# The state's two products moved onto 32-column groups of the array, in one row with the products of scores and v

## The chip, the cores and the metric

The kernel runs on one core of one Trainium2 chip. The metric is the time of one execution on the device, in microseconds; smaller is better. The kernel before took 1318.28 us as the median of three runs (1317.63 to 1319.15).

## The reference

The input `x` has 8 sequences of 1024 tokens with 256 features, in float32. It is normalised, and two things that read the normalised `xn` are added to it: a linear attention with 16 heads of 16 features, and a mixture of 8 experts of which each token uses 2.

```
q = elu(xn @ Wq.T) + 1 ; k = elu(xn @ Wk.T) + 1 ; v = xn @ Wv.T        # 16 heads of 16
kv_cumsum = cumsum over tokens of k[d] * v[e]                          # per head, 16 x 16
k_cumsum  = cumsum over tokens of k
out   = sum over d of q[d] * kv_cumsum[d, e]
denom = clip(sum over d of q[d] * k_cumsum[d], 1e-6)
x + (out / denom) @ Wo.T + sum over the 2 chosen experts of weight * (silu(xn @ W1) * (xn @ W3)) @ W2
```

The running sum `kv_cumsum` is what this change is about. It is never formed token by token. The tokens are cut into chunks of 128; within a chunk the masked scores q.k are multiplied with v, and what all earlier chunks of the sequence contribute is q times a state, the sum of k times v over those chunks.

## The kernel before

The 8192 tokens form 16 blocks of 512 tokens (two blocks to a sequence), and each block has four chunks of 128. Features lie across partitions in two halves (`KC` = 2, index `hh`), each with 8 heads, or 4 pairs of heads of 32 features (`PAIR`). Everything is float32, and one float32 matmul of the program appears in the profile as two records.

The experts' work is cut into tiles of 128 tokens that share an expert. The main loop has one iteration for each such tile, 132 in all. An iteration fetches the tile's rows and the expert's weights ahead of time, multiplies with W1 and W3 (`gu_ps`, L1216, 16 matmuls), transposes the next tile (`xg_t`, L1183), and multiplies the previous tile with W2 (`y_ps`, L1235). Ahead of this the iteration makes one step of the attention, sometimes two (`attend_upto`). Each block has nine steps: four that project q, k and v and prepare the denominator, one for the first chunk's scores, and four in which `block_steps` calls `scores` of the next chunk, `attend` of the last one (the product with Wo, `a_ps`, L979) and `weigh` of the present one. Two steps are made together only at certain places of a block (`TOGETHER`).

`scores(t, c)` multiplies k and q (`s_ps`, L919, on groups of 32 rows of the array, 8 matmuls) into four banks; VectorE masks each bank for causality (L926) and so frees it. Then, unless the chunk is the last of its sequence, it multiplies k and v (`kv_ps`, L934): two matmuls, one for each half, with 128 columns of k held in the array and 128 columns of v streamed. Of each 128 by 128 result only the 16 by 16 squares on the diagonal, one for each head, are wanted; VectorE multiplies with the mask `heads` (L939) and adds the state so far (L941), and the sum is the new state. The old state, `before_c`, goes with the chunk.

`weigh(t, c, ...)` fills one result `o_ps` of 128 partitions by 2 x 128. First come the products of q and the old state (L953): two matmuls over the whole array. Onto them it adds the products of masked scores and v (L960): 16 matmuls of 32 columns each, one column group for each pair of heads in a half, so that four of them stand side by side in the array. VectorE multiplies with the reciprocal denominator (L967) into `oT`.

Results of the array lie in three pools of banks: four for `s_ps` and `gu_ps`, two for `y_ps` and `a_ps`, and two for `kv_ps`, `o_ps` and the transposes. The start of the kernel (up to the first iterations) is written in a fixed order; after it, a scheduler decides the order of the instructions on TensorE, VectorE and ScalarE, within each engine's queue, and the engines work their queues in order. Weight transfers are issued from SP, in the order of the program.

Of the kernel before, what the change touches and what calls it, by code (L numbers as in the profile page):

```python
# [46 lines left out]
F32 = mybir.dt.float32  # L47
# [3 lines left out]
ALU = mybir.AluOpType  # L51
AX = mybir.AxisListType

P = 128
# [3 lines left out]
PAIR = 2 * HD  # L58
# [5 lines left out]
def tile_attention_moe(  # L64
# [14 lines left out]
    nc = tc.nc  # L79
    B, L, H = x.shape  # L80
    E, _, I = w1.shape
    KC = H // P
    IC = I // P
    TB = 512
    NCH = TB // P
    N = B * L
    NBLK = N // TB
    BLK_PER_SEQ = L // TB
# [22 lines left out]
    three = ctx.enter_context(tc.tile_pool(name="three", bufs=3))  # L111
# [3 lines left out]
    ps_t = ctx.enter_context(tc.tile_pool(name="ps_t", bufs=2, space=bass.MemoryType.PSUM))  # L115
# [114 lines left out]
    heads = const.tile([P, P], F32, name="heads")  # L230
# [16 lines left out]
    va = const.tile([P, NCH, HALF, 2, PAIR], F32, name="va")  # L247
# [12 lines left out]
        nc.gpsimd.tensor_copy(own_of[:, o, o * HALF : (o + 1) * HALF], own)  # L260

    causal_b = causal.unsqueeze(1).to_broadcast([P, 4, P])
    heads_b = heads.unsqueeze(1).to_broadcast([P, KC, P])


    lgs = {}
# [116 lines left out]
    new = f_one.tile([P, E, MOST], F32, name="new")  # L383
# [384 lines left out]
    def own_v(va, c, a, b):  # L768

        pairs = va[:, c, a:b].rearrange("p g s d -> p g (s d)")  # L770
        return pairs.rearrange("p g (q d) -> p g q d", d=HD)[:, :, 0:4:3, :]
# [135 lines left out]
    state = [None]  # L907

    def scores(t, c):

        qT, qm, kT, kn, va, rden = blocks[t]
        first = t % BLK_PER_SEQ == 0 and c == 0
        last = t % BLK_PER_SEQ == BLK_PER_SEQ - 1 and c == NCH - 1
        span = bass.ts(c, P)
        s_ps = [ps_mm.tile([P, KC, 2, P], F32, tag="mm", name="s_ps") for r in range(4)]
        for hh in range(KC):
            for r in range(4):
                rows = slice(32 * r, 32 * r + 32)
                nc.tensor.matmul(  # L919
                    s_ps[r][:, hh].rearrange("p a l -> p (a l)"), lhsT=kT[rows, hh, span],  # L920
                    rhs=qm[rows, hh, :, span], start=True, stop=True,
                )
        s_sb = []
        for r in range(4):
            sm = masked.tile([P, KC * 2, P], F32, tag="s_sb", name="s_sb")
            nc.vector.tensor_tensor(  # L926
                sm, s_ps[r].rearrange("p k a l -> p (k a) l"), causal_b, ALU.mult
            )
            s_sb.append(sm)
        before_c = state[0]  # L930
        if not last:
            kv_ps = ps_t.tile([P, KC, P], F32, tag="t", name="kv_ps")
            for hh in range(KC):
                nc.tensor.matmul(  # L934
                    kv_ps[:, hh, :], lhsT=kn[:, c, bass.ts(hh, P)],
                    rhs=own_v(va, c, 4 * hh, 4 * hh + 4), start=True, stop=True,
                )
            new = three.tile([P, KC, P], F32, tag="kv", name="kv")
            nc.vector.tensor_tensor(new, kv_ps, heads_b, ALU.mult)  # L939
            if not first:  # L940
                nc.vector.tensor_tensor(new, new, before_c, ALU.add)  # L941
            state[0] = new
        return t, c, s_sb, before_c

    def weigh(t, c, s_sb, before_c):

        qT, qm, kT, kn, va, rden = blocks[t]
        first = t % BLK_PER_SEQ == 0 and c == 0
        span = bass.ts(c, P)
        o_ps = ps_t.tile([P, KC, P], F32, tag="t", name="o_ps")  # L950
        if not first:
            for hh in range(KC):
                nc.tensor.matmul(  # L953
                    o_ps[:, hh, :], lhsT=before_c[:, hh, :], rhs=qT[:, hh, span],
                    start=(hh == 0), stop=False, skip_group_check=True,
                )
        for hh in range(KC):
            for a in range(2):
                for r in range(4):
                    nc.tensor.matmul(  # L960
                        o_ps[32 * r : 32 * r + 32, hh, :],
                        lhsT=va[:, c, 4 * hh + r, a, :],
                        rhs=s_sb[r][:, 2 * hh + a, :],
                        start=(first and a == 0), stop=(a == 1), skip_group_check=True,
                    )
        oT = two.tile([P, KC, P], F32, tag="oT", name="oT")
        nc.vector.tensor_tensor(oT, rden[:, c], o_ps, ALU.mult)  # L967
        return oT

    ats = {}  # L970
# [24 lines left out]
    def block_steps(t):  # L995


        for i, _ in enumerate(project(t)):
            if i == 1 and behind:
                attend(*behind.pop())  # L1000
            if i in (1, 3, 5, 8):
                yield
        if t + 1 < NBLK:
            fetch(t + 1)
        waiting = scores(t, 0)
        yield
        done = None
        for c in range(NCH):
            coming = scores(t, c + 1) if c + 1 < NCH else None
            if done and c + 1 < NCH:  # L1010
                attend(*done)
            oT = weigh(*waiting)
            if done and c + 1 == NCH:
                attend(*done)
            done = t, c, oT
            waiting = coming
            if c + 1 < NCH or t + 1 < NBLK:
                yield
        behind.append(done)
        if t + 1 == NBLK:  # L1020
            attend(*behind.pop())
            yield
# [24 lines left out]
    with tc.manual_schedule(engines={EN.DVE, EN.Activation, EN.PE, EN.Pool}):  # L1047
# [63 lines left out]
        for _ in range(2):  # L1111
            idle_ps = ps_mm.tile([P, TB], F32, tag="mm", name="idle_ps")
            nc.tensor.matmul(
                idle_ps, lhsT=ident, rhs=blocks[0][0][:, 0, :], start=True, stop=True
# [170 lines left out]
    for j in range(NM + 1):  # L1285
        if j + 1 < NM:
            ffn_norm(j + 1)
        t = FB + j
# [27 lines left out]
        if LISTS <= j < LISTS + NBLK - FB:  # L1316
            t = FB + j - LISTS
# [66 lines left out]
```

## Time and profile before

| what | value |
|---|---|
| median of three runs | 1318.28 us |
| profiled execution, whole | 1329.68 us |
| its span | 1328.0 us |
| granted TensorE clock, mean | 0.989 |
| TensorE busy in the span | 1270.6 us, 96% |
| VectorE busy | 636.9 us, 48% |
| ScalarE busy | 526.1 us, 40% |
| GpSimd busy | 523.1 us, 39% |
| `kv_ps`, L934: 224 records | 40.0 us busy |
| `o_ps` from the state, L953: 224 records | 34.9 us busy |
| `o_ps` from scores and v, L960: 2048 records | 73.2 us busy |
| `s_ps`, L919: 1024 records | 85.5 us busy |

PE is TensorE's matmul side and PEld its weight loads, which run beside the matmuls; DVE is VectorE, ACT ScalarE, POOL GpSimd. A line of the timeline gives the start of a group of equal instructions, its duration, the engine, the line of the code, the operation with its result and operands, the number of rows by columns of the array in use, the moving operand (partitions by elements) and the count; in brackets, the engine's idle time before it and what ended that. The ends of matmuls are modelled and overlap with what follows, so that distances between starts tell more than durations.

### The profile page before, as it was taken

The page shows a single profiled execution, that of the slowest core. Times are in us where ns is not written, and L with a number is a line of the kernel's source. Part 1 is how long each engine was busy: PE and PEld are TensorE (multiplying, and loading weights), DVE is VectorE, ACT ScalarE, POOL GpSimd, SP SyncE. Part 2 cuts the span into 40 slices and gives each one's busy share as a digit, 9 for nine tenths or more (in the row PEclk, how much of TensorE's full clock was granted, in tenths as well). Part 3 has the DMA queues.
Part 4 walks back from the last instruction along what each step waited for, and adds up shares of the span by engine and source line. Part 5 has one row for each costly group of instructions (what it writes and reads, how often), then busy time and mean ns, then how long its engine had stood idle before and what let it go on. Part 6 is the DMA issues. An engine that isn't in the chain of part 4 may idle for free.

```text
span 1328.0 us, 28290 instructions
## 1 busy us (share of the span) xinstructions
PE 1270.6 (96%) x10968; PEld 1092.2 (82%) x10968; DVE 636.9 (48%) x1436; ACT 526.1 (40%) x1060; POOL 523.1 (39%) x460
## 2 busy tenths in 40 slices
PE   5689999999999999999999999999999999999996
PEld 4478887787888888888888888898888888888886
DVE  7667489764252434435343535344443525243441
ACT  4466364461524325161525243341515152433411
POOL 3633333233254443443443525343434334343432
PEclk9899999999999999999999999999999999999998
DMA  9688576466685766666675757476676767575763
GB/s 340 229 276 258 154 200 170 130 173 206 176 229 141 198 166 155 189 173 172 169 190 145 216 132 208 126 188 171 160 186 170 189 153 194 147 198 134 198 161 72
DMA packets 163462, 240.36 MB, mean 181 GB/s; under 512 B 16098, under 2 KB 87394, under 8 KB 163042
## 3 DMA queue, kind: packets, MB, share of 16 engines
q1 hardware_dynamic: 119938, 184.31, 45.0%
q0 software_dynamic: 38064, 43.22, 19.3%
q10 hardware_dynamic: 5328, 11.01, 2.3%
q8 instruction: 90, 1.47, 0.5%
q14 instruction: 42, 0.34, 0.1%
HBM read 196.30 MB, written 52.67 MB: 187 GB/s over the span
## 4 chain that ended last, share of the span: by engine, by line
PE 87%; DVE 7%; ACT 2%; issue 1%; DMA 1%; another core or an unknown queue 1%; POOL 0%; POOLq 0%; DVEq 0%; ACTq 0%
PE gu_ps L1216 34%; PE y_ps L1235 16%; PE o_ps L960 5%; PE s_ps L919 5%; PE a_ps L979 4%; PE zq L795 4%; PE zkk L811 4%; PE zkv L811 4%; PE kv_ps L934 2%; PE o_ps L953 2%; PE xg_t L1183 2%; DVE s_sb L926 1%; PE tp L333 1%; PE den L880 1%; PE tp L858 1%
## 5 line engine op out<-in xcount | busy, mean ns | idle before, releaser
L1216 PE MATMUL gu_ps<-xgT,w 128*128 128x128 f32 x4224 | 511.2, 278 | 8.9 <-DVE s_sb L926 7.6
L1216 PEld LDWEIGHTS gu_ps<-xgT,w 128*128 128x128 f32 x4224 | 492.5, 193 | 28.8 <-issue 12.5
L1162 POOL DMA_INDIRECT xg<-in_x_dram,src_i x132 | 128.1, 970 | 406.1 <-ACT xgT L1185 322.4
L1246 POOL DMA_INDIRECT out_dram<-y,dst_i x107 | 176.3, 1648 | 222.2 <-DVE kn L765 54.2
L1235 PE MATMUL y_ps<-w_sb,hT 128*128 x1056 | 250.6, 380 | 2.6 <-DVE hT L1227 2.0
L1227 DVE TENSOR_TENSOR hT<-gu_ps,hT 128x512 f32<-128x512 f32 x132 | 91.1, 690 | 274.4 <-PE gu_ps L1216 198.0
L1235 PEld LDWEIGHTS y_ps<-w_sb,hT 128*128 128x128 f32 x1056 | 190.2, 190 | 24.0 <-DVE hT L1227 1.9
L1224 ACT ACTIVATE hT<-gu_ps 128x512 f32<-128x512 f32 x132 | 78.8, 597 | 299.9 <-PE gu_ps L1216 255.0
L926 DVE TENSOR_TENSOR s_sb<-s_ps,causal 128x512 f32<-128x512 f32 x256 | 163.6, 684 | 54.0 <-PE s_ps L919 25.5
L1242 DVE TENSOR_SCALAR y<-y_ps,entry 128x256 f32<-128x256 f32 x132 | 63.5, 481 | 120.0 <-PE y_ps L1235 75.0
L1167 POOL DMA_INDIRECT entry<-tab_d,of_i x107 | 106.5, 995 | 32.6 <-issue 30.5
L1185 ACT COPY xgT<-xg_t 128x256 f32<-128x256 f32 x132 | 49.0, 371 | 145.2 <-PE xg_t L1183 141.7
L984 ACT COPY at<-a_ps 128x256 f32<-128x256 f32 x64 | 23.7, 370 | 159.2 <-PE a_ps L979 149.0
L919 PE MATMUL s_ps<-qm,kT 32*128 32x256 f32 x1024 | 85.5, 405 | 0.5 <-DVE hT L1227 0.4
L1174 ACT ACTIVATE xg<-xg,entry 128x256 f32<-128x256 f32 x132 | 79.6, 603 | 3.4 <-issue 3.4
L960 PE MATMUL o_ps<-s_sb,va 128*32 128x128 f32 x2048 | 73.2, 276 | 0.0
L919 PEld LDWEIGHTS s_ps<-qm,kT 32*128 32x128 f32 x1024 | 51.0, 184 | 24.2 <-issue 19.6
L979 PE MATMUL a_ps<-wo_sb,oT 128*128 128x256 f32 x256 | 69.0, 393 | 0.1
L1246 POOL DMA_INDIRECT acc_d<-y,src_i x25 | 44.0, 1761 | 55.2 <-DVE y L1242 15.4
L960 PEld LDWEIGHTS o_ps<-s_sb,va 128*32 128x32 f32 x2048 | 53.2, 109 | 9.8 <-DVE oT L967 0.8
L811 PE MATMUL zkk<-wkv_sb,xnT 128*128 128x256 f32 x256 | 60.0, 384 | 0.0
L795 PE MATMUL zq<-xnT,wq_sb 128*128 128x512 f32 x128 | 59.9, 609 | 0.0
(211 smaller groups left out, 1361.7 us busy)
## 6 DMA issues: line engine op xcount, KB each, us to landing
w<-in_w_dram SPq DMA_DIRECT2D x264, 512.0 KB
den_d<-over SPq DMA_DIRECT2D x64, 128.0 KB
rden<-den_d SPq DMA_DIRECT2D x16, 512.0 KB
xnT_d<-xnT ACTq DMA_DIRECT2D x15, 512.0 KB
xnT<-xnT_d SPq DMA_DIRECT2D x15, 512.0 KB
out_dram<-in_x_dram SPq DMA_DIRECT2D x12, 512.0 KB
out_dram<-at POOLq DMA_DIRECT2D x12, 512.0 KB
xb<-in_x_dram SPq DMA_DIRECT2D x10, 512.0 KB
```

What stands on the lines that cost most here:

```text
L795: nc.tensor.matmul(z, lhsT=wq_sb[:, k, bass.ts(o, P)], rhs=xnTs[t][:, k, :], start=(k == 0), stop=(k == KC - 1),)
L811: nc.tensor.matmul(z[:, i, :], lhsT=xnTs[t][:, k, bass.ts(c + i, P)], rhs=wkv_sb[:, k, a, :], start=(k == 0), stop=(k == KC - 1),)
L919: nc.tensor.matmul(s_ps[r][:, hh].rearrange("p a l -> p (a l)"), lhsT=kT[rows, hh, span], rhs=qm[rows, hh, :, span], start=True, stop=True,)
L926: nc.vector.tensor_tensor(sm, s_ps[r].rearrange("p k a l -> p (k a) l"), causal_b, ALU.mult)
L960: nc.tensor.matmul(o_ps[32 * r : 32 * r + 32, hh, :], lhsT=va[:, c, 4 * hh + r, a, :], rhs=s_sb[r][:, 2 * hh + a, :], start=(first and a = ...
L979: nc.tensor.matmul(a_ps, lhsT=oT[:, hh, :], rhs=wo_sb[:, hh, :], start=(hh == 0), stop=(hh == 1),)
L1162: nc.gpsimd.indirect_dma_start(out=xg[j], out_offset=None, in_=x_rows[:, :], in_offset=bass.IndirectOffsetOnAxis(ap=src_i[:, i : i + 1], a ...
L1167: nc.gpsimd.indirect_dma_start(out=entry[j], out_offset=None, in_=table[:, :], in_offset=bass.IndirectOffsetOnAxis(ap=num_i[:, i : i + 1], ...
L1216: done = nc.tensor.matmul(ps[:, i, :], lhsT=w13[:, k, bass.ts(i, P)], rhs=xgT[j][:, k, :], start=(k == 0), stop=(k == KC - 1),)
L1227: nc.vector.tensor_tensor(hT, gu[1], hT, ALU.mult)
L1235: done = nc.tensor.matmul(y_ps, lhsT=hT[:, i, :], rhs=w2_sb[:, bass.ds(e * (IC * H) + i * H, H)], start=(i == 0), stop=(i == IC - 1),)
L1246: nc.gpsimd.indirect_dma_start(out=rows[:, :], out_offset=bass.IndirectOffsetOnAxis(ap=dst_i[:, i : i + 1], axis=0), in_=ys.pop(j), in_off ...
```

## The change

The product of k and v moves from `scores` to `weigh`, behind the products of scores and v, and is computed only where it is wanted: for each pair of heads, 32 columns of k against the 32 columns of v of the same pair, eight matmuls in place of two, each on its own group of 32 columns of the array. The result has 2 x 32 columns in place of 2 x 128 and shares one tile, and one bank, with `o_ps`. VectorE spreads it over 128 columns while it multiplies with the mask. The product of q and the old state is likewise cut into eight matmuls of 32 columns. The state is now read and replaced within `weigh`; the instructions of VectorE for the new state stand behind the one that makes `oT`.

```diff
@@ scores
-        before_c = state[0]
-        if not last:
-            kv_ps = ps_t.tile([P, KC, P], F32, tag="t", name="kv_ps")
-            for hh in range(KC):
-                nc.tensor.matmul(
-                    kv_ps[:, hh, :], lhsT=kn[:, c, bass.ts(hh, P)],
-                    rhs=own_v(va, c, 4 * hh, 4 * hh + 4), start=True, stop=True,
-                )
-            new = three.tile([P, KC, P], F32, tag="kv", name="kv")
-            nc.vector.tensor_tensor(new, kv_ps, heads_b, ALU.mult)
-            if not first:
-                nc.vector.tensor_tensor(new, new, before_c, ALU.add)
-            state[0] = new
-        return t, c, s_sb, before_c
+        return t, c, s_sb
@@ weigh
-        o_ps = ps_t.tile([P, KC, P], F32, tag="t", name="o_ps")
+        both_ps = ps_t.tile([P, KC * P + KC * PAIR], F32, tag="t", name="o_ps")
+        o_ps = both_ps[:, 0 : KC * P].rearrange("p (k l) -> p k l", k=KC)
+        kv_ps = both_ps[:, KC * P :].rearrange("p (k d) -> p k d", k=KC)
+        before_c = state[0]
         if not first:
             for hh in range(KC):
-                nc.tensor.matmul(
-                    o_ps[:, hh, :], lhsT=before_c[:, hh, :], rhs=qT[:, hh, span],
-                    start=(hh == 0), stop=False, skip_group_check=True,
-                )
+                for r in range(4):
+                    nc.tensor.matmul(
+                        o_ps[32 * r : 32 * r + 32, hh, :],
+                        lhsT=before_c[:, hh, 32 * r : 32 * r + 32], rhs=qT[:, hh, span],
+                        start=(hh == 0), stop=False, skip_group_check=True,
+                    )
...
+        if not last:
+            for hh in range(KC):
+                for r in range(4):
+                    nc.tensor.matmul(
+                        kv_ps[32 * r : 32 * r + 32, hh, :],
+                        lhsT=kn[:, c, hh * P + 32 * r : hh * P + 32 * r + 32],
+                        rhs=own_v(va, c, 4 * hh + r, 4 * hh + r + 1),
+                        start=True, stop=True, skip_group_check=True,
+                    )
         oT = two.tile([P, KC, P], F32, tag="oT", name="oT")
         nc.vector.tensor_tensor(oT, rden[:, c], o_ps, ALU.mult)
+        if not last:
+            new = three.tile([P, KC, P], F32, tag="kv", name="kv")
+            nc.vector.tensor_tensor(
+                new.rearrange("p k (g d) -> p k g d", d=PAIR),
+                kv_ps.unsqueeze(2).to_broadcast([P, KC, 4, PAIR]),
+                heads.rearrange("p (g d) -> p g d", d=PAIR).unsqueeze(1).to_broadcast(
+                    [P, KC, 4, PAIR]
+                ),
+                ALU.mult,
+            )
+            if not first:
+                nc.vector.tensor_tensor(new, new, before_c, ALU.add)
+            state[0] = new
         return oT
```

## The prediction

> **What bounds the kernel now.** I read the page's busy times and slices first, then the busy times of a long stretch, then TensorE's waits, then its timeline around one chunk.
>
> ```profile
> PE 1270.6 (96%) x10968; PEld 1092.2 (82%) x10968; DVE 636.9 (48%) x1436; ACT 526.1 (40%) x1060; POOL 523.1 (39%) x460
> 400.00:1280.00 880.00, 875.90 (x7630) 764.21 (x7632) 371.39 (x654) 329.63 (x600) 360.68 (x298) 1.00 0.66 172
> PE gu_ps L1216 <- DVE s_sb L926: 4.8, 7, 1.2
> PE gu_ps L1216 <- issue: 0.8, 5, 0.2
> ```
>
> The second line is the stretch from 400 to 1280 us (PE, PEld, DVE, ACT, POOL, clock, DMA share, GB/s): TensorE works 875.9 of 880 us at full clock. The last two lines are the longest of TensorE's waits between 300 and 1290 us; all of them come to 7.1 us, none on a transfer. So in this stretch a nanosecond taken off TensorE's stream is a nanosecond off the kernel, unless the next instruction then waits for something. A chunk looks like this:
>
> ```profile
> 613.18 1.15 PE L919 MATMUL s_ps<-qm,kT 32*128 32x256 f32 x16
> 614.26 0.71 PE L934 MATMUL kv_ps<-va,kn 128*128 128x128 f32 x4
> 614.81 1.03 PE L979 MATMUL a_ps<-wo_sb,oT 128*128 128x256 f32 x4
> 615.67 0.61 PE L953 MATMUL o_ps<-qT,kv 128*128 128x128 f32 x4
> 616.21 1.08 PE L960 MATMUL o_ps<-s_sb,va 128*32 128x128 f32 x32
> ```
>
> (start, duration, group; a program matmul is two records; gate and up, L1216, follow at 617.22.) Names below: s, K, a, S, W for these five, g for L1216. The durations overlap, so I price by starts: K holds the stream 0.548 us (614.257 to 614.806), S 0.538, W 1.011. Read record by record, full-array records start every 0.111 us, and W starts packs of four records, one for each group of 32 columns, every 0.109 us. Where the form of the array changes, time is lost: 0.106 us more in a first 128-wide group after s, 0.095 from the full array to W's columns, 0.024 for W's first load, 0.115 from columns back to the full array.
>
> **What the Trainium skill says.** "TensorEngine Tiling (Array Packing)", section Key Properties: "Changing tiling mode (not just tile) drains the TensorE". The trace agrees (0.1 to 0.2 us per change, above). "TensorE: Matmul & The Clock Gate", section LDWEIGHTS, says that a load takes the number of columns divided by 1.2 ns, whatever the rows; the trace agrees: after a change of form the second load starts 0.108 us after the first at 128 columns and 0.029 us at 32. The same page, Back-to-back issue gap, gives some 25 ns as the least distance of two matmuls however small; the trace shows four records of different column groups starting within 20 ns, so I take that price for one group's own stream, and keep its other reading as a rival.
>
> **The change, part by part.**
>
> *K.* Removed: two matmuls of 128 columns by 128 moving (4 records, 4 x 0.111 = 0.442 us). Added: eight of 32 columns by 32 moving, 16 records, four packs, behind W in the same form of the array. No record of that shape exists in the trace. Bounds: from below the load, since a pack of four 32-column loads can follow another so:
>
> ```profile
> 616.21 0.13 PEld L960 LDWEIGHTS o_ps<-s_sb,va 128*32 128x32 f32 x4
> 616.21 0.16 PEld L960 LDWEIGHTS o_ps<-s_sb,va 128*32 128x32 f32 x8
> 29.58 0.29 PE L449 MATMUL cnt_ps<-run,ones 128*128 128x8 f32 x2
> ```
>
> The first line is the timeline cut at 616.23, the second cut at 616.26: four loads, then eight, so the second pack is 0.029 us behind the first. The third shows that a short moving side doesn't hold the array: two matmuls of 8 columns whose starts (29.582 and 29.613) are 0.031 apart. 32 moving columns are a quarter of 128, 0.109 / 4 = 0.027, so load and stream ask the same, 0.029. K's cost is then 4 x 0.029 = 0.117 us. From above: four packs at the pace of W, 4 x 0.109 = 0.436. I take 0.117: K saves 0.325 us.
>
> *S.* Two matmuls become eight with the same moving side: four packs x 0.109 = 0.436 against 0.442, 0.006 saved. Its gain is the form of the array: S, W and K now stand in one.
>
> *Where K stood.* All 56 K groups of the timeline, by what follows them. (1) Before a, 22, and once before the transpose: the change of form after s falls on a instead, S enters columns as W did; saving 0.325 + 0.006 = 0.331 each, 23 x 0.331 = 7.6. (2) Directly before S or W, 18 (first and second chunk of a block): s, full array, columns becomes s, columns. By starts s+K+S+W is 1.076 + 0.548 + 0.540 + 1.011 = 3.175; after it is 1.076 + 0.024 + 0.436 + 0.872 + 0.117 + 0.115 = 2.640. Saving 0.53 each, 18 x 0.53 = 9.5. (3) Directly before g, 15: there g needs the bank that VectorE's masking of s has to free first.
>
> ```profile
> 598.16 0.71 PE L934 MATMUL kv_ps<-va,kn 128*128 128x128 f32 x4
> 598.34 2.42 DVE L926 TENSOR_TENSOR s_sb<-s_ps,causal 128x512 f32<-128x512 f32 x4
> 599.02 1.64 PEld L1216 LDWEIGHTS gu_ps<-xgT,w 128*128 128x128 f32 x14 [0.34 <-DVE s_sb L926]
> ```
>
> g starts at 599.02 when the first of the four maskings (0.68 us, from 598.34) ends; without K TensorE only waits longer. 14 of the 15 wait so (K to g is 0.73 to 1.96 us instead of 0.548); they gain nothing, and K's new place costs 0.117: 14 x 0.117 = 1.6 lost, 0.3 gained in the fifteenth.
>
> *Order.* In the changed program the places where two steps run together read K, five matmuls of g, a, S, W in place of W, S, part of W, one of g, rest of W: six changes of form become four, 0.32 us less, five times: 1.6.
>
> *VectorE.* The same three instructions, oT (0.41 us), K's mask (0.42) and the running sum (0.43), now in this order behind W. The mask reads 256 elements with repeats from a bank as before, so about 0.42 stays; at half the speed it would be 0.8. The four maskings of s stand ahead of them, and the fourth waits for W's end in both kernels, so VectorE is done 0.68 + 0.41 + 0.42 + 0.43 = 1.94 us behind W. What is queued behind: hT, which waits for g's end, 3.7 us behind W; 1.7 us of cover. The running sum is next read by S one step later, some 8 us; only where two steps run together does it come close: K 0.12, change 0.2, five g 1.1, a 0.87, 2.3 us against 1.94. Hidden, by 0.35 us. If that cover is gone, S waits by the difference, at about six places. K and o share one bank now, so of the two banks for such results one is held about 0.8 us longer; the other goes to the transposes, and the held one is next asked for a step later.
>
> *ScalarE, GpSimd, SP.* No instruction or DMA of theirs is added or dropped; weights arrive ahead (no wait on them), at a DMA share of 0.66, and a 1.3% faster TensorE asks for 0.67.
>
> Sum: 7.6 + 9.5 - 1.6 + 0.3 + 1.6 = 17.4 us. The profiled execution took 1329.68 us (span 1328.0), which gives 1312.3; the runs' median, 1318.28, is 11.4 lower, the same program with the same TensorE stream, so I subtract from it: 1300.9, rounded to **1301**. Before 350 us TensorE has idle time and a scheduler reorders more; I allow 3 us either way.
>
> **Rivals.**
> *Packs don't get shorter.* If a pack of small matmuls can't follow faster than W's 0.109 us, or each record needs the 25 ns of the skill (16 x 0.025 = 0.40), K costs 0.40 to 0.44. Then (1) gives about 0.2 to 1.1, (2) 18 x 0.21 to 0.25 = 3.7 to 4.4, (3) -6.2 to -5.6, order 1.6: a sum of -0.7 to +1.5, so 1317 to 1319. For it: W's mean is 27 ns per record. Against: eight loads within 50 ns.
> *TensorE's instruction stream becomes the bound* (the slower end). "TensorE: Matmul & The Clock Gate", Step-by-step, names 62 ns per matmul where decoding is done in software. K's eight would take 0.496, 0.38 more than forecast, 56 x 0.38 = 21.3: 1322. W's sixteen take 1.011 us, 63 ns each with the changes, so the trace doesn't exclude it by rate. Against: at 616.47 TensorE's queue already stands at the semaphore of the g that starts at 617.22, so it runs 0.75 us ahead, and K's eight at 62 ns would use up 0.38 of it. It decides where K costs more than about 0.43.
> *S waits for the running sum.* Two steps together, VectorE late: at most 1.9 us uncovered at six places, 11 us: 1312. For: VectorE takes its instructions in order, oT stands ahead. Against: five matmuls of g and a in between.
> That g's wait in case (3) shrinks too, because VectorE is less crowded, would give up to 14 x 0.33 = 4.6 more: 1296; but the first masking doesn't stand behind K's mask today.
>
> **How the numbers follow.** Forecast 0.78, packs as slow as W's 0.11, instruction stream 0.05, late sum 0.06. The forecast's own range is 1296 to 1307: the early part's 3 us, K between 0.06 and 0.2 (56 x 0.08 = 4.5). 8 in 10 takes in the late sum: 1295 to 1313; the two slow cases stay out. Within 0.2% (2.6 us) is about what a measurement of this kernel can't tell from no change: faster 0.78 + 0.06 = 0.84, same 0.11, slower 0.05.
>
> **What would show it.** The new K packs should have mean starts 0.03 us apart and K behind W hold the stream 0.1 to 0.15 us before what it cost to leave columns; S to W no more than 0.44; s to S about 0.13 us less a full visit to the 128-wide form. At the 14 places of case (3) the time from s's start to g's start should stay what it was (2.15 us from 596.87 to 599.02 above), with TensorE's wait for the masking longer; this is the step that I could have too dear. It is wrong if K's groups are 0.4 us, if S waits on the running sum, or if the span falls by less than these groups do.

## The result, and the profile after

The changed kernel takes 1300.25 us as the median of four runs (1298.38 to 1301.42), the kernel before 1318.72 (four runs, 1317.63 to 1319.84). The ratio is 0.9853, with an interval of 0.9839 to 0.9867: 18.5 us less. Measured again later it was 1300.36 against 1321.06, a ratio of 0.9835 (0.9815 to 0.9856). The forecast was 1301.

The busy times of the changed kernel's page and of the stretch from 400 to 1250 us (PE, PEld, DVE, ACT, POOL, clock, DMA share, GB/s), and all of TensorE's waits in that stretch (total us, times, longest):

```profile
PE 1240.7 (96%) x12312; PEld 1069.7 (83%) x12312; DVE 635.5 (49%) x1436; ACT 526.1 (41%) x1060; POOL 524.1 (40%) x460
400.00:1250.00 850.00, 841.31 (x8448) 736.19 (x8442) 364.49 (x644) 326.20 (x593) 358.06 (x295) 1.00 0.66 176
PE gu_ps L1229 <- DVE s_sb L923: 4.6, 7, 0.7
PE gu_ps L1229 <- issue: 4.0, 5, 0.8
```

TensorE has 29.9 us less of busy time, though 1344 records more, and still sets the end. Its waits in this stretch come to 8.6 us, all of them at 12 places ahead of gate and up, where K no longer stands (case 3 of the prediction). VectorE, ScalarE and GpSimd have the same work as before.

A chunk with a between s and S (case 1 of the prediction) in the timeline of the changed kernel; s, K, a, S, W and g are the prediction's names:

```profile
605.07 1.15 PE L916 MATMUL s_ps<-qm,kT 32*128 32x256 f32 x16
606.15 1.13 PE L992 MATMUL a_ps<-wo_sb,oT 128*128 128x256 f32 x4
607.21 0.65 PE L942 MATMUL o_ps<-qT,kv 128*32 128x128 f32 x16
607.67 1.06 PE L950 MATMUL o_ps<-s_sb,va 128*32 128x128 f32 x32
608.55 0.31 PE L960 MATMUL o_ps<-va,kn 128*32 128x32 f32 x16
608.78 3.84 PE L1229 MATMUL gu_ps<-xgT,w 128*128 128x128 f32 x32
```

By starts S holds the stream 0.46 us (0.024 for the first load and 0.437 for four packs), W 0.873, K 0.237. Without the change of form behind it, 0.115, K is 0.122 us for its 16 records. The same timeline, cut at 608.605, at 608.635 and at 608.665, shows its packs:

```profile
608.55 0.24 PE L960 MATMUL o_ps<-va,kn 128*32 128x32 f32 x8
608.55 0.28 PE L960 MATMUL o_ps<-va,kn 128*32 128x32 f32 x12
608.55 0.31 PE L960 MATMUL o_ps<-va,kn 128*32 128x32 f32 x16
```

Each 0.03 us brings four more: the packs start at 608.546, 608.574, 608.606 and 608.638. Within the first pack the four records start at 608.546, 608.553, 608.559 and 608.565.

Case 2, where K stood between s and S: the first two lines are from the first profile of before (s, then g, with K, S and W between them), the last two from the changed kernel (with S, W and K between them).

```profile
531.67 1.15 PE L919 MATMUL s_ps<-qm,kT 32*128 32x256 f32 x16
534.85 0.82 PE L1216 MATMUL gu_ps<-xgT,w 128*128 128x128 f32 x5
515.44 1.15 PE L916 MATMUL s_ps<-qm,kT 32*128 32x256 f32 x16
518.09 1.16 PE L1229 MATMUL gu_ps<-xgT,w 128*128 128x128 f32 x8
```

From s to g it was 3.175 us and is 2.649.

Case 3, where g follows s directly, is in the next lines; the line of VectorE is its four maskings.

```profile
507.13 0.64 PE L879 MATMUL den<-ksum,own_of 128*32 128x128 f32 x16
507.71 1.36 PE L916 MATMUL s_ps<-qm,kT 32*128 32x256 f32 x16
509.04 2.42 DVE L923 TENSOR_TENSOR s_sb<-s_ps,causal 128x512 f32<-128x512 f32 x4
509.73 1.94 PE L1229 MATMUL gu_ps<-xgT,w 128*128 128x128 f32 x15 [0.66 <-DVE s_sb L923]
```

From the start of s to the start of g are 2.02 us. With K between them it was the same 2.02 us (518.70 to 520.71 in the second profile of before, e5, whose lines are shown there). At five of the 12 places the profile names no cause ("issue" above). There, too, g starts just behind the first masking: from the start of s, at 652.06, that masking ends after 1.85 us and g starts after 1.95.

**Which two profiles can be compared.** The profiled execution of before that the prediction worked from took 1329.68 us, 11 above the runs; that of the changed kernel (1298.38) lies among its runs. The difference of those two spans, 31.6 us, is therefore not the effect of the change. A second profile of before (experiment e5) has a span of 1319.8, and against two profiles of the changed kernel (1296.4 and 1299.7) gives 23.4 and 20.1.

**The granted clock.** Executions of one kernel also differ because the granted TensorE clock drops for a while. The lines are the same 3.4 us in two profiles of the changed kernel, which has the same order of work in both; the second line is from e9 (columns as in the second line at the top of this section: us, PE, PEld, DVE, ACT, POOL, clock, DMA share, GB/s).

```profile
129.60:133.00 3.40, 3.40 (x55) 2.15 (x59) 3.15 (x11) 1.08 (x4) 1.73 (x2) 1.00 0.75 193
129.60:133.00 3.40, 3.40 (x28) 2.19 (x25) 2.25 (x6) 0.27 (x1) 1.16 (x2) 0.51 0.75 193
```

TensorE is busy in both, but at a clock of 0.51 it gets through 28 records in place of 55. I call 3.4 us at about half the clock a dip. In every trace of this case the dips lie ahead of the 400th us, apart from the last 8 us. One costs at most 1.7 us (half of 3.4); the two that e9 has more than the first profile lengthened their iterations by 1.57 and 1.62. The spread of the runs goes the same way: of the 33 runs of before that were made beside e1, those with a mean granted clock of 0.992 took 1316.04 to 1316.84 us, those with 0.990 took 1319.43 to 1322.27. Why the clock drops is not shown.

### The profile page after: what moved, and what is told of

Its sections match the earlier page's. It is cut to its first block, busy times and chain, and to the rows that moved or that the text cites. A ratio compares the mean times of both kernels' runs of the same rounds, so it can differ in the third digit from the quotient of the medians.

```text
span 1296.4 us, 31016 instructions
## 1 busy us (share of the span) xinstructions
PE 1240.7 (96%) x12312; PEld 1069.7 (83%) x12312; DVE 635.5 (49%) x1436; ACT 526.1 (41%) x1060; POOL 524.1 (40%) x460
## 4 chain that ended last, share of the span: by engine, by line
PE 88%; DVE 9%; issue 1%; DMA 1%; POOL 0%; ACT 0%; POOLq 0%; DVEq 0%; ACTq 0%
PE gu_ps L1229 36%; PE y_ps L1248 17%; PE a_ps L992 5%; PE s_ps L916 4%; PE o_ps L950 4%; PE zq L794 4%; PE zkk L810 4%; PE zkv L810 4%; PE o_ps L942 2%; PE xg_t L1196 2%; PE tp L857 1%; PE tp L332 1%; DVE st L282 1%; DVE at_place L572 1%; DVE s_sb L923 1%
## 5 line engine op out<-in xcount | busy, mean ns | idle before, releaser
L950 PE MATMUL o_ps<-s_sb,va 128*32 128x128 f32 x2048 | 69.1, 273 | 0.0
L992 PEld LDWEIGHTS a_ps<-wo_sb,oT 128*128 128x128 f32 x256 | 44.7, 190 | 23.8 <-issue 14.2
```

The lines of the kernel that those rows point to most:

```text
L950: nc.tensor.matmul(o_ps[32 * r : 32 * r + 32, hh, :], lhsT=va[:, c, 4 * hh + r, a, :], rhs=s_sb[r][:, 2 * hh + a, :], start=(first and a = ...
L992: nc.tensor.matmul(a_ps, lhsT=oT[:, hh, :], rhs=wo_sb[:, hh, :], start=(hh == 0), stop=(hh == 1),)
```

## The experiments

All kernels do the full computation. Times are medians. A stretch that I use throughout goes from the product with W2 of tile 30 (about 390 us) to that of tile 131 (about 1285 us), where the order of TensorE's groups repeats from block to block and where no trace has a dip of the clock. In it before takes 910.1 us (e5), the changed kernel 896.9. An iteration goes from one tile's product with W2 to the next tile's.

**e1: K alone.** S goes back to the whole array.

```diff
-                for r in range(4):
-                    nc.tensor.matmul(
-                        o_ps[32 * r : 32 * r + 32, hh, :],
-                        lhsT=before_c[:, hh, 32 * r : 32 * r + 32], rhs=qT[:, hh, span],
+                nc.tensor.matmul(
+                    o_ps[:, hh, :], lhsT=before_c[:, hh, :], rhs=qT[:, hh, span],
...
```

> K (k times v) in 32-column groups behind W as in the changed kernel; S (q times the old state) back to two matmuls of 128 columns. Theory (K's shorter stream is most of the gain, the form of the array the rest): against the changed kernel a visit to the 128-wide form comes back at the 18 places of case 2, 18 x 0.2 = 3.6 us, and 0.3 for S itself: about 1304 us. Rival (the gain is the form of the array, all three products in one): about 1316.

1299.3 us, a ratio to before of 0.9857 (0.9834 to 0.9881); the stretch took 898.2. K alone brings nearly all of it, and the rival falls. The 3.6 us that I expected S to cost were too many: with S whole, a visit to the 128-wide form comes back only where S stands directly behind s. In e1's trace that is so at 7 places, not 18; at eight of the 18 the chunk is the first of its sequence and has no S. The timeline shows such a place of e1:

```profile
657.94 1.15 PE L916 MATMUL s_ps<-qm,kT 32*128 32x256 f32 x16
659.02 0.71 PE L941 MATMUL o_ps<-qT,kv 128*128 128x128 f32 x4
659.66 1.08 PE L948 MATMUL o_ps<-s_sb,va 128*32 128x128 f32 x32
660.55 0.31 PE L958 MATMUL o_ps<-va,kn 128*32 128x32 f32 x16
```

S and W together hold 1.54 us (659.02 to 660.55; 0.642 + 0.897), against 0.461 + 0.873 = 1.33 in the changed kernel: 0.205 per place, as priced (0.2). With 0.008 at the other chunks the stretch (6 such places, some 36 others) should differ by 1.5, and differs by 1.3. In the whole time this part of the change, some 2 us, is not resolved.

**e2: S alone.** The kernel before, with S in columns and K untouched.

```diff
-                nc.tensor.matmul(
-                    o_ps[:, hh, :], lhsT=before_c[:, hh, :], rhs=qT[:, hh, span],
+                for r in range(4):
+                    nc.tensor.matmul(
+                        o_ps[32 * r : 32 * r + 32, hh, :],
+                        lhsT=before_c[:, hh, 32 * r : 32 * r + 32], rhs=qT[:, hh, span],
...
```

> The kernel before with S alone cut into eight matmuls of 32 columns; K stays whole and in its old place. Theory: as many changes of form as before at most places, some 2 us less where two steps run together: 1316 to 1318.5 us. Rival (the form of the array): 1310 or less.

1315.66 us, ratio 0.9958 (0.9946 to 0.9971); the stretch 908.0, 2.1 less than before, of which 1.8 lie at the five places where two steps run together (0.36 each). The stretch is as the theory said, the median 0.3 us below its range and far from the rival's 1310; columns for S alone do little, because K still calls for the whole array.

**e3: the move alone.** K and S as wide as before, K behind W.

```diff
...
+                nc.tensor.matmul(
+                    kv_ps[:, hh, :], lhsT=kn[:, c, bass.ts(hh, P)],
+                    rhs=own_v(va, c, 4 * hh, 4 * hh + 4),
...
```

> K and S whole (128 columns), K only moved behind W, its bank shared with o. Theory: nothing at cases 1 and 2, and at case 3, where K stood in a wait of g for nothing, K now costs 0.44 each, 14 x 0.44 = 6.2: about 1325 us, slower than before. Rival (the gain comes from the order: VectorE freed ahead of the maskings, state later): about 1310, faster than before.

1320.2 us, ratio 1.0004 (0.9994 to 1.0015): no difference, neither the 1310 of the rival nor the 1325 of the theory. The mechanism is there: in case 3 g starts no earlier without K.

```profile
663.82 1.15 PE L916 MATMUL s_ps<-qm,kT 32*128 32x256 f32 x16
665.78 3.81 PE L1220 MATMUL gu_ps<-xgT,w 128*128 128x128 f32 x32 [0.81 <-issue]
```

1.96 us from s to g, as in before with K in between (670.13 to 672.09). My expectation left out two savings. Where two steps run together, the moved K lets matmuls of g and a stand between the two chunks, and five such iterations get shorter by 0.53 us each, 2.65 in all. And where a chunk has no S, s, K, W with the 128-wide K between two narrower forms becomes s, W, K: 0.19 us less at each of six places, 1.15 in all. The cost is 0.45 us for each of 13 K's in the stretch (12 that stood in g's wait, and one that moved in from the iteration ahead of it): 5.85 - 2.65 - 1.15 = +2.05, and the stretch is +2.0 (912.1). The first 400 us made up the rest of the total; that part I didn't take apart.

**e4: K in columns, but streaming all of v.**

```diff
-                        rhs=own_v(va, c, 4 * hh + r, 4 * hh + r + 1),
+                        rhs=own_v(va, c, 4 * hh, 4 * hh + 4),
```

> As the changed kernel, but each of K's eight matmuls streams all 128 columns of v instead of its own pair's 32 (VectorE's mask as before the change). Theory: a pack costs 0.109 in place of 0.029, K 0.436 in place of 0.117, 56 x 0.32 = 17.9 us more: about 1318. Rival (forms of the array): 1301 to 1303.

1318.46 us, ratio 0.9985 (0.9974 to 0.9996), as the theory said to half a microsecond. The timeline:

```profile
606.99 1.06 PE L950 MATMUL o_ps<-s_sb,va 128*32 128x128 f32 x32
607.87 0.62 PE L960 MATMUL o_ps<-va,kn 128*32 128x128 f32 x16
608.42 3.84 PE L1224 MATMUL gu_ps<-xgT,w 128*128 128x128 f32 x32
```

K holds 0.550 us instead of 0.237, 0.313 more. In the stretch there are 43 such groups, 43 x 0.313 = 13.5, and it lost 13.5 (910.4); in the whole time 56 x 0.313 = 17.5 stand against 18.2. The forms of the array are those of the changed kernel, so the gain of the change is the 32 moving columns. The forms do save something, by the measured savings and K's price in e4 some 5 us in the stretch (12 x 0.21 in case 2 and 5 x 0.53 where two steps run together, an estimate); but a K that costs 0.43 in place of a wait (12 x 0.43 in case 3) takes as much again.

**e5: before, once more.**

> The kernel before, unchanged, for a second profile: its profiled execution on record took 1329.68 us, 11 above its other runs, while that of the changed kernel (1298.38) lies among its own. Theory (that one execution lost time that others don't lose): profile near 1319, and the places at which TensorE's g after s began late because VectorE began the clamp of the denominator late (five of eight) are fewer. Rival (the profiler itself costs 11 us): again about 1330 with the same places.

1319.22 us, and its profiled execution took 1321.48: the profiler doesn't cost 11 us, and the first profile of before was an unlucky execution. In it VectorE began to clamp the denominator (`over`) late at six of the eight places after 350 us where the denominator's products stand directly ahead of s, by up to 0.9 us, and g started up to 1.2 us later. First a place of the first profile:

```profile
522.76 0.64 PE L880 MATMUL den<-ksum,own_of 128*32 128x128 f32 x16
524.08 0.29 DVE L886 TENSOR_SCALAR over<-den 128x128 f32<-128x128 f32 x1 [4.18 <-PE den L880]
525.96 1.27 PE L1216 MATMUL gu_ps<-xgT,w 128*128 128x128 f32 x9 [0.63 <-DVE s_sb L926]
```

The same place in e5:

```profile
518.12 0.64 PE L880 MATMUL den<-ksum,own_of 128*32 128x128 f32 x16
518.83 0.29 DVE L886 TENSOR_SCALAR over<-den 128x128 f32<-128x128 f32 x1 [3.57 <-PE den L880]
520.71 1.49 PE L1216 MATMUL gu_ps<-xgT,w 128*128 128x128 f32 x11
```

1.32 us from the products to the clamp against 0.71. The lost time is 4.4 us over the eight places, and another 4.8 were lost before the first tile's product with W2 (72.0 against 67.2 us), where that execution has one dip of the clock more (63.9 to 67.4 us). Why VectorE was late in that execution I don't know: at four places the clamp ended within 0.02 us of the end of one of GpSimd's scatters, but at others they overlap freely. In the other profiles of this order of work the clamp follows the products within 0.06 us of the usual time.

**e6: the first chunk's K back behind s.**

```diff
+        if c == 0:
+            kv_tile = ps_t.tile([P, KC * PAIR], F32, tag="t", name="kv_ps")
+            kv_ps = kv_tile.rearrange("p (k d) -> p k d", k=KC)
...
```

> As the changed kernel, but for the first chunk of each block K (32 columns, in a tile of its own) stands right behind s again, where g waits for VectorE's masking. Theory: K is hidden in that wait at about 14 places, 14 x 0.12 = 1.7 us less than the changed kernel: about 1298.6. Rival (the wait isn't one, K costs the same anywhere): 1300.3 or more.

1300.81 us, ratio 0.9861 (0.9841 to 0.9882): not the 1298.6. In the stretch it is right: 895.2 against 896.9, and the 12 iterations there that lost their K are 0.12 us shorter each. But from the first tile to tile 30 it took 326.3 us against 319.9 of the changed kernel (323.0 in its second profile). The scheduler set the groups of the first 400 us in another order, and there are four dips of the clock against one (three in the second profile): three dips more are up to 5.1 of the 6.3 us. The four runs have a mean clock of 0.988 to 0.990, those of the changed kernel in the result 0.991 or 0.992. The median shows the sum, and so doesn't confirm the theory by itself.

**e7: other work into g's wait.** The first chunk's s ahead of the denominator and of the projection of v.

```diff
-        for c in range(0, NCH, 2):
-            if t > 0:
-                for _ in project_v(t, c):
-                    pass
-            yield
+        waiting_of[t] = scores(t, 0)
...
         yield
+        for c in range(0, NCH, 2):
+            if t > 0:
+                for _ in project_v(t, c):
+                    pass
+        yield
         del xnTs[t]
```

> As the changed kernel, but the first chunk's s stands ahead of the denominator's products and of the projection of v, so that these two lie between s and g. Theory (g waits 0.7 to 0.9 us for the first masking of s at 13 to 15 places): about 0.68 us less at each of 13, 8.8 in all: about 1291.5 us. Rival (the wait moves to the projection of v, which takes banks of the same pool, or the denominator comes late): 1299 to 1303.

1299.35 us, ratio 0.9849 (0.9824 to 0.9874): by the median the rival was right. The trace says otherwise: the stretch took 889.5 us, 7.3 less than the changed kernel, and from the first tile to tile 30 it took 328.2, 8.3 more. Again the order there is another, and again there are four dips of the clock against one, up to 5.1 us. All four runs have a low mean clock, 0.986 to 0.989, where the 23 runs of before made beside them have 0.989 to 0.992. Whether the order brings the dips is not shown.

**e8: the same from the fourth block on**, so that the first 400 us keep their order.

```diff
-            if i in (1, 3, 5, 8):
+            if i in ((1, 3, 5, 8) if t < 3 else (1, 3, 5, 6)):
...
-        waiting = scores(t, 0)
+        waiting = waiting_of.pop(t) if t >= 3 else scores(t, 0)
```

> As the changed kernel, but from the fourth block on s of the first chunk stands ahead of the denominator's products and of the projection of v (the first three blocks keep their order; TensorE's order differs at these 13 places alone). Theory (g waits 0.7 to 0.9 us for the first masking, and the earlier trial lost its gain in the first 400 us): 9.81 us from the projection to the end of g and the next two groups becomes 9.04, less 0.09 for one change of form, 13 x 0.68 = 8.8 us less than the changed kernel of the same call: about 1291.5 us. Rival (TensorE's gain comes back as a wait elsewhere): within 2 us of the changed kernel.

1290.35 us, ratio to before 0.9778 (0.9755 to 0.9802); the changed kernel, measured beside it (e9), took 1300.36. That is 10.0 us less than the changed kernel and the fastest of all. The timeline of e8 around the place:

```profile
501.73 1.15 PE L924 MATMUL s_ps<-qm,kT 32*128 32x256 f32 x16
502.80 0.64 PE L882 MATMUL den<-ksum,own_of 128*32 128x128 f32 x16
503.63 3.72 PE L811 MATMUL zkv<-wkv_sb,xnT 128*128 128x256 f32 x16 [0.19 <-DVE s_sb L931]
507.19 3.73 PE L1237 MATMUL gu_ps<-xgT,w 128*128 128x128 f32 x32
```

The masking now runs beside the denominator and the projection; 0.19 us of waiting is left of 0.66. Against the first profile of the changed kernel the iterations at the 13 places are shorter by 0.68 us (eight places) or 0.77 (the five where the profile named no cause), 9.3 in all where I expected 8.8. At two other places a now waits for oT, 1.2 us together, a part of what the rival said. Net that is some 8 us; the stretch, with 12 of the places, took 889.4 against 896.8. So the wait that took K's gain in case 3 is shown by its removal, and at all the places. The remaining 2 of the 10.0 us are not shown to come from it: the profiled executions of e8 and e9 differ by 3.6 us before the 140th us, where both have the same order and e9 has two dips of the clock more. Runs with the same mean clock, 0.992, took 1288.49 and 1289.81 us in e8, 1297.51 and 1298.07 in e9, some 8.6 apart.

**e9: the changed kernel again.**

> The changed kernel, unchanged, on the same chip and in the same rounds as the one before it: 1300 us, profile within 2 us of the one on record, and again no place where VectorE begins the clamp of the denominator late.

1300.36 us; the profiled execution took 1301.53 (1298.38 the first time), and the stretch 896.8 (896.9). Two clamps are 0.05 or 0.06 us late, no other. Of the 3.3 us between the two spans 3.2 are two iterations ahead of tile 30 in which the same groups took 1.6 us longer, each with a dip of the clock that the first profile doesn't have (129.5 and 238.7 us).

## Why the prediction was right

*TensorE is the bound.* Right: in the stretch the time followed the stream, +13.5 us in e4 for 13.5 added, +1.3 in e1 for 1.5. In the medians, which take in the first 400 us, the same changes came out within some 3 us (+18.2 for 17.5 and -1.0 for +2).

*K's cost, 0.117 us.* Measured 0.122 (0.237 less 0.115 for the change of form behind it). The lower bound was the right one: packs start 0.028 to 0.032 us apart. What sets this pace is not shown: the load of four 32-column groups (0.029 us), the stream of 32 columns (0.027 by W's pace) and the starts of four records one behind the other (4 x 0.0065 = 0.026) lie too close together. The rival that takes W's pace or the 25 ns of the Trainium skill ("TensorE: Matmul & The Clock Gate", Back-to-back issue gap) for every record falls: 16 records in 0.122 us are 7.6 ns each. That price holds for one column group at most, here 0.03 us. The rival of the instruction stream falls by the same number, 0.122 / 8 = 15 ns for each matmul of the program, and because TensorE waits nowhere behind K in the stretch.

*S, and the changes of form.* S took 0.461 us with the first load, forecast 0.460. A chunk whose S follows s: s, S, W, K take 1.076 + 0.461 + 0.873 + 0.238 = 2.648, forecast 2.640. The 18 places of case 2 were not all alike, as the prediction's sum took them to be: at eight there is no S, and s, K, W went from 2.73 to 2.21, 0.52 less, so that the sum held all the same; two of the 18 K's stood behind the product with W2, not behind s. With a in between, K + a + S + W took 0.548 + 0.866 + 0.538 + 1.011 = 2.963, and a + S + W + K takes 1.061 + 0.461 + 0.873 + 0.237 = 2.632: 0.331 less, forecast 0.331. The Trainium skill ("TensorEngine Tiling (Array Packing)", Key Properties) says that a change of the tiling mode drains TensorE; in each of these numbers a change of form costs 0.1 to 0.2 us.

*Case 3.* g starts 2.02 or 1.96 us behind s with K (e5) or without it, at all 13 places after 350 us in the first profile of the changed kernel; in its second profile two of them are 0.05 later. e8 shows the cause. The 2.15 us that the prediction read, and K to g of up to 1.96, came from the late clamps of the one execution (2.02 and 0.73 to 0.88 in e5); its range also leaves out the first block's place, 3.47. As K is free in a wait of any length, the sum doesn't change.

*The running sum.* The rival that S waits for it falls: in the long stretch S has no wait on VectorE. It was the other way round: it is the kernel before in which S waits for it, twice in the first 405 us, 1.9 us in the first profile and 1.8 in e5, whose line is this:

```profile
PE o_ps L953 <- DVE kv L939: 1.8, 2, 1.3
```

The changed kernel has no such line, but a new one of 2.0 us, a waiting once for oT, so that this cancels.

*The sizes that were off.* The order where two steps run together saved about 0.53 us at each of five places, not 0.32: +1.0. From tile 30 to 131 the prediction's terms give 12.5 (18 x 0.331 + 12 x 0.53 - 12 x 0.117 + 1.6), with that correction 13.5; measured 13.2 and 13.3 against e5. Ahead of tile 30 the terms give the remaining 4.9; from the first tile to tile 30 I measured 10.3 in the first profile of the changed kernel and 7.2 in e9. The clock accounts for that spread: e5 and e9 have three dips there, the first profile has one, and two dips are up to 3.4 us. With equal dips the excess over the terms is 2.3. TensorE's waits from 60 to 405 us come to about the same (13.6 us in e5, 13.3 and 13.2 in the changed kernel), while the order of the groups differs; which of them saved the time, I leave open. I had allowed 3. By spans the sum is 20.1 to 23.4 where 17.4 was forecast; by medians 18.5 the first time and 20.7 the second. So the terms came out some 3 us short, and that the first median lies within 0.75 us of the forecast is in part luck.

*The profiled execution.* Subtracting from the median was right; had I forecast the span of a profile from that execution, 1310.6, I would have missed the two of the changed kernel by 14.2 and 10.9.

## What to carry to other kernels

Where only a block diagonal of a product is wanted, cut it so that each column group streams its own block alone: the gain is the shorter moving side (e4). A group that stands in another engine's wait costs nothing there and something wherever it is moved to; look for such waits before moving, and fill them (e8). If a scheduler orders the instructions, compare kernels by a stretch whose order is the same in both, and compare the granted clock before you give a difference to the order: in e6 and e7 the whole time hid effects that the stretch showed, and much of what hid them was the clock.

## What was not expected of the hardware

Records of four column groups can be issued densely enough that 16 matmul records and 16 loads pass in 0.122 us, under 4 ns each, with no wait of TensorE behind them. The granted clock can fall to half for 3.4 us while TensorE is busy throughout (129.6 to 133.0 us in e9), and not in another execution of the same kernel. And one execution among many can lose some 10 us, spread over several places: the first profile of before against e5, where 3.3 us of it lie in the stretch, at full clock (1.00).
